# A gated block of two attentions: half of the second head's K moved ahead of a wait, VectorE's sums put behind pairs of GpSimd's, and two constants of the order's planner

## The chip, the cores and the metric

The kernel runs on one core of a Trainium2 chip. The core has five engines that work side by side, each through its own list of instructions in order: TensorE (PE in the profile, with PEld for its weight loads), VectorE (DVE), ScalarE (ACT), GpSimd (POOL), and SyncE (SP), which here only starts transfers. The metric is the time of one execution on the device in microseconds (us), lower is better. The kernel before takes 4916.66 us (median of three runs, 4911.18 to 4921.75).

## The reference

For each of 8 batches, x is 1024 rows of 512 and the context is 1024 rows of 384, all in float32. The block is two attentions one behind the other, each behind a layernorm and each added to x.

```python
x = x + tanh(g_xattn) * xattn(layernorm(x), ctx)   # 8 heads of 64, K and V from the context
x = x + tanh(g_ffn)   * ffn(layernorm(x))          # 16 heads of 32, K and V from x itself

# xattn: softmax(q k^T / 8) v, then @ Wo + bo
# ffn:
q_norm   = q / norm(q, axis=-1)
q_scaled = (q_norm + query_embedding) * softplus(temperature)
h   = softmax(q_scaled k^T / sqrt(32)) v
out = h * gates(h)      # gates: softmaxes of h @ Wr.T, top 3 of 15, and of h @ Ws.T
return out @ Wp.T + bp
```

## The kernel before

**Tiling.** The 512 columns of q and k are cut into 4 chunks of 128, each with 2 heads of 64 (kind 1, the first attention) or 4 heads of 32 (kind 2, the second). In each batch the chunks of kind 1 come first, then `between` finishes the first attention, forms the second's layernorm and its transpose y2T and starts the projections, and then the chunks of kind 2 run. Inside a batch they are called one, two, three and the fourth in the code. The 1024 query columns are handled in two halves of 512, `h` = 0 and 1.

**One chunk.** Four kinds of work belong to it:
- *Projections* (L319 to L395): q and k of each half, four products of four column tiles each (`MM`, one product of the inner loop, is planned at 950 ns). For kind 2 the norm of q follows: ScalarE adds the bias (qq, L355), GpSimd squares it (rn, L356), TensorE sums the squares over a head (pn, L379), ScalarE forms the inverse root (L380, L381), GpSimd multiplies (L382), ScalarE scales (L389).
- *Maxima* (L406 to L472): bfloat16 copies of k and q are made by GpSimd (kb, qb, L398), TensorE forms the scores a first time in bfloat16 (pm, L413), and VectorE takes each row's maximum (mx, L454; L437 in the wide form, which `pace` uses). The maxima then go through a transpose (pr, L465) and a small transfer into the row `sh`, from which the shift of the softmax is added by a product with ones. A chunk of kind 2 has 32 steps of maxima ("pairs") and two closing steps.
- *Scores and values* (L478 to L512, L587 to L626): TensorE forms shift plus scores (sc, L500), ScalarE takes the exponential into a tile e of 128x1024 (L511), TensorE multiplies by v (av, L598). A chunk of kind 2 has 8 steps per half, each with two e tiles, u = 0 and 1.
- *Sums* of the softmax. GpSimd adds two e tiles (`paired`, L516). The result is either added by VectorE to a running sum (L529) or kept as a further term. TensorE then adds up all terms that were kept, with a product by ones (sum, L549). So a result that VectorE does not take costs TensorE time instead. At most 5 e tiles may be held as terms (`room`, L677); when they are too many, the oldest waiting sum is emitted at once (`now`), and if none waits, TensorE sums what there is into a part (L562).

**The order.** The order on TensorE, ScalarE, VectorE and GpSimd is the order in which the program emits instructions. While it emits, it keeps planned clocks: `at["PE"]`, `at["DVE"]` and `at["POOL"]`, in ns, moved on by a planned duration at each instruction (`pe`, `dve`, `pool`). Work that should not be emitted yet waits in two lists, `soon` and `later`, each item with a planned due time; `due` (L666) emits from the head of each list what is due. A sum of VectorE goes into `later` with GpSimd's planned end of that addition (L517, L518).

**The pacing.** During the scores of a chunk, `attend` (L717) mixes in the maxima of the next chunk (and of the one after it, `ahead`) and fillers such as projections. `pair` (L705) emits one step of maxima only where VectorE's planned clock is not too far ahead of TensorE's. `in_time` (L744) compares the planned work of the maxima still to do with the time left in the chunk. Where it says no, VectorE takes no sums in chunks of kind 2 (`ontime`, used in `add` at L523), and TensorE has to sum instead. `pace` (L1049) does the same between the two attentions, where no scores run.

**Around the change.** `between` (L992): the output projection of the first attention for 8 row tiles, each followed by layernorm, a round trip through memory (`put`, `get`) and VectorE's transpose into y2T (`turn`, L1011; L242). The first chunk's projection is begun while the last three tiles are still being turned (L1031 to L1036): q and k of half 0 need tiles 0 to 3 alone, q and k of half 1 need tiles 4 to 7. Then come the first tile of V (L1037, L1038), the rest of the first chunk's projection (L1039), and, in `pace`, the projections of the second and third chunk and the rest of V.

Of the kernel before, what the change touches and what calls it, by code (L numbers as in the profile page):

```python
# [21 lines left out]
def tile_gated_block(  # L22
# [41 lines left out]
    NT = N // P  # L64
    ND = D // P
# [15 lines left out]
    work = ctx.enter_context(tc.tile_pool(name="work", bufs=2))  # L81
# [174 lines left out]
    at = {"PE": 0.0, "DVE": 0.0, "POOL": 0.0}  # L256
    WIDE, MM, PAIR, FOUR, TR, SUM, EXP = 700, 950, 300, 350, 800, 1000, 2100
# [12 lines left out]
    def dve(ns):  # L270
        at["DVE"] = max(at["DVE"], at["PE"]) + ns
# [24 lines left out]
    class Chunk:  # L296
# [19 lines left out]
            if "q" in what:  # L316
                self.wq = load_wc(wq, self.c, f"wq_{self.key}")

        def project(self, st):  # L319

            self.q = qk.tile([P, N], F32, tag="q", name=f"q_{self.key}", bufs=3)
            self.k = qk.tile([P, N], F32, tag="k", name=f"k_{self.key}", bufs=3)
            self.qb = qk.tile([P, N], BF16, tag="qb", name=f"qb_{self.key}")
            self.kb = qk.tile([P, N], BF16, tag="kb", name=f"kb_{self.key}")
            self.waiting = True
            halves = range(NH)
            if self.kind == 1:
                for h in halves:
                    yield from self.project_k(st, h)
                soon.append((at["PE"] + 3000, self.copied, self.kb, self.k))  # L330
                for h in halves:
                    yield from self.project_q(st, h)
            else:
                for h in halves:
                    yield from self.project_q(st, h)
                    yield from self.project_k(st, h)
                    yield from self.norms(h)
                soon.append((at["PE"] + 1000, self.copied, self.kb, self.k))
            soon.append((at["PE"] + 3000, self.begin_maxima))
# [180 lines left out]
        def add(self, h, s, u, a, last):  # L520

            accs = self.acc.setdefault((h, u), [])
            wanted = self.kind == 1 and self.b or ontime[0]  # L523
            free = at["DVE"] <= at["PE"] + 1000
            if accs and not forced[0] and not (wanted if free else wanted and last):
                later.insert(0, (at["PE"] + 300, self.add, h, s, u, a, last))
                return
            elif accs and wanted:
                nc.vector.tensor_tensor(accs[-1], accs[-1], a, ALU.add)  # L529
                dve(1750)  # L530
                live[0] -= 1
                ready = at["DVE"] + 500
            else:
                accs.append(a)
                ready = at["PE"]
            if last and s + 1 == self.ns:
                later.append((ready, self.summed, h, True))
# [49 lines left out]
        def value(self, step):  # L587

            h, s = step
            width, st = self.width, self.st  # L590
            if s == 0:
                self.av = ps_av.tile([P, H], F32, tag="av", name=f"av_{self.key}_{h}")
            e = self.e[step]
            for kk in range(self.nk):
                kc = s * self.nk + kk
                for i in range(self.nh):
                    j = kk * self.nh + i
                    nc.tensor.matmul(  # L598
                        self.av[ts(i, width), :],
                        lhsT=st.v[:, kc, ts(self.c * self.nh + i, width)],  # L600
                        rhs=e[j // 2][:, j % 2, :],
                        start=(kc == 0),
                        stop=(kc == NT - 1),
                    )
                pe(1000)
                if kk == 0 and self.kind == 1:
                    room(1, self, h)
                    self.paired(h, s, 0, e[0], e[1], True)
                if kk + 1 < self.nk:
                    yield  # L610
            if self.kind == 2 and s + 2 == self.ns and self.ends:
                for u in range(2):
                    self.whole[h, u] = [e[u], self.e[h, s + 1][u]]
                live[0] += 4
                later.append((at["PE"] + 3000, self.summed, h, True))
            elif self.kind == 2 and s % 2 == 0:
                room(2, self, h)
                for u in range(2):
                    self.paired(h, s + 1, u, e[u], self.e[h, s + 1][u], u == 1)
            if s == self.ns - 1:  # L620
                nc.scalar.copy(st.hT[h][:, self.c, :], self.av)
                self.divided(h)
            if s % 2 or self.kind == 1:
                self.e.pop(step)
                self.e.pop((h, s - 1), None)
            yield "valued"  # L626
# [27 lines left out]
    later, soon = [], []  # L654
# [34 lines left out]
    def beside(a, b, n=1):  # L689

        while a or b:
            for g in [a] * n + [b]:
                if g and next(g, "end") == "end":
                    a, b = (None if g is a else a), (None if g is b else b)
                elif g:
                    yield

    def run(g, ns):

        end = at["PE"] + ns  # L700
        while g and at["PE"] < end:
            if next(g[0], "end") == "end":
                g.pop(0)
# [13 lines left out]
    def attend(  # L717
        ch, after, first, fillers, cost, maxima=None, ahead=None, since=0.0, rate=1.1, least=300
    ):

        filled, attended = 0.0, 0.0
        columns[0] = ch.width
        total = len(ch.steps) * (ch.SC + 1000 * ch.nk)

        def fill():
            nonlocal filled
            was = at["PE"]  # L730
            while fillers:
                if next(fillers[0], "end") == "end":
                    fillers.pop(0)
                elif ch.kind == 2 or not part[0]:
                    break
            filled += max(at["PE"] - was, least if at["PE"] - was < MM else 0)

        def pairs(slack):
            due(at["PE"])
            if maxima and maxima.mx:  # L740
                return pair(maxima, slack)
            return bool(ahead and ahead.done + 3 < ahead.pairs and pair(ahead, slack))

        def in_time(share):  # L744

            if not maxima or not (maxima.mx or maxima.waiting):
                return True
            pairs = maxima.pairs - maxima.done
            work = pairs * 1450 + 1750 + max(0, at["DVE"] - at["PE"])
            steps = (1 - share) * len(ch.steps) * (2 if ch.kind == 2 else 3)  # L750
            return pairs < 2 or pairs <= steps - 3 and work <= (1 - share) * (1.1 * total + cost) - 7000

        was = at["PE"]
        for got in ch.attention(after, first):
            attended += at["PE"] - was
            share = max(0, attended / total - since) / (1 - since)
            ontime[0] = in_time(attended / total)
            due(at["PE"])
            if got == "begun":
                fill()  # L760
            while got == "valued" and fillers and filled < cost * min(1, rate * share):
                pairs(0)
                fill()
            pairs(1100)
            while got == "ready" and (maxima.mx or maxima.waiting or fillers):
                if not pairs(1100):
                    if fillers:
                        fill()
                    else:
                        at["PE"] += 100  # L770
            was = at["PE"]
        if fillers and since:
            due(1e12)
        run(fillers, 1e9)
        columns[0] = HD2
# [73 lines left out]
    def v2(st):  # L849
        for t in range(NT):  # L850
            ps = gen(f"pv2_{st.b}_{t}")
            yield from product(
                ps, lambda k, t=t: st.yT[:, k, ts(t, P)], lambda k: st.wv[:, k, :], ND
            )
            nc.scalar.copy(st.v2[:, t, :], ps)  # L855
            nc.gpsimd.tensor_tensor(st.v2[:, t, :], st.v2[:, t, :], bv_b, ALU.add)  # L856
            pool(1270)
            yield
# [133 lines left out]
    def between(st, nxt):  # L992
# [25 lines left out]
        one, two, three = st.chunks[2][0:3]  # L1018
# [14 lines left out]
        three.loads()  # L1033
        for t in range(NT - 3, NT):
            turn(t)
            run(fill, 3 * MM)  # L1036
        values = v2(st)  # L1037
        run([values], ND * MM)  # L1038
        run(fill, 1e9)  # L1039
        fill = [two.project(st), beside(values, put1(nxt), ND) if nxt else values]  # L1040
        if nxt:
            fill.append(fetch(nxt, wv1, "wv1"))
        fill.append(three.project(st))
# [135 lines left out]
```

## Time and profile before

| | before |
|---|---|
| time, median of 3 runs | 4916.66 us (4911.18 to 4921.75) |
| time of the profiled execution | 4917.12 us |
| its span, first to last instruction | 4915.3 us |
| TensorE busy | 4754.1 us (97%) |
| VectorE busy | 3112.0 us (63%) |
| GpSimd busy | 2567.6 us (52%) |
| ScalarE busy | 2254.5 us (46%) |
| mean granted TensorE clock | 0.989 |

How to read the lines: a group of instructions is named by its line in the kernel, its engine and its operation, then out<-in with shapes, the count, its busy time and the mean duration of one, and the idle time of the engine just before. A line of the waits gives who waited for whom, then total us, how many times, and the longest. A line of a timeline gives the start in us, the duration in us of a run of like instructions, and in brackets the idle time before it with what ended it. A line of a table by stretches gives the stretch, its length, the busy time and count of instructions, the granted TensorE clock (1.00 is full), the share of transfers and their rate. One product of four column tiles in float32 shows as 8 matmul records.

### The profile page before, as it was taken

How to read it: one execution, taken by the hardware profiler on the slowest of the kernel's cores; microseconds unless marked ns; L12 is line 12 of the kernel's file. 1: busy time of each engine (PE TensorE's matmuls, PEld its weight loads, DVE VectorE, ACT ScalarE, POOL GpSimd, SP SyncE). 2: the span in 40 equal slices, each digit the busy share in tenths (PEclk: the TensorE clock that was granted, in tenths of full speed). 3: DMA queues.
4: the chain of work that ended last, by engine and by line, in shares of the span. 5: the costliest groups of instructions: out<-in, count | busy, mean ns of one | idle time of the engine just before them, and what ended most of it. 6: DMA issues, size and time to landing. Idle time of an engine off the chain costs nothing.

```text
span 4915.3 us, 83941 instructions
## 1 busy us (share of the span) xinstructions
PE 4754.1 (97%) x35196; PEld 1422.8 (29%) x35196; DVE 3112.0 (63%) x4225; ACT 2254.5 (46%) x2916; POOL 2567.6 (52%) x1346
## 2 busy tenths in 40 slices
PE   9999999999999999999999999999999999999998
PEld 2222232222322223222232222322223222232232
DVE  4557665576656865557655576555765567655664
ACT  3435634355343553435534355343552436524364
POOL 1635646366363663636636366363663636636474
PEclk9999999999999999999999999999999999999999
DMA  2020010200103001030010300102002020010100
GB/s 80 27 94 23 26 50 27 95 24 24 50 27 103 16 24 50 29 102 14 24 59 24 99 14 24 65 22 95 14 24 66 26 90 14 17 52 28 34 1 18
DMA packets 212683, 208.12 MB, mean 42 GB/s; under 512 B 24144, under 2 KB 147024, under 8 KB 212304
## 3 DMA queue, kind: packets, MB, share of 16 engines
q1 hardware_dynamic: 212016, 202.76, 13.0%
q8 instruction: 275, 4.51, 0.4%
q14 instruction: 104, 0.85, 0.1%
q10 hardware_dynamic: 288, 0.00, 0.0%
HBM read 153.93 MB, written 48.23 MB: 41 GB/s over the span
## 4 chain that ended last, share of the span: by engine, by line
PE 77%; DVE 12%; issue 3%; POOL 3%; ACT 2%; DMA 2%; SPq 1%; DVEq 0%; ACTq 0%; POOLq 0%
PE sc L500 20%; PE av L598 17%; PE po L282 9%; PE pq L282 8%; PE pm L413 7%; PE pk L282 6%; PE pv L282 5%; DVE mx L454 4%; DVE mx L437 4%; PE sum L549 4%; DVE e L529 3%; POOL e L516 2%; ACT e L511 1%; PE pn L282 1%; SPq L469 1%
## 5 line engine op out<-in xcount | busy, mean ns | idle before, releaser
L516 POOL TENSOR_TENSOR e<-e,e 128x1024 f32<-128x1024 f32 x764 | 1859.3, 2449 | 1122.9 <-PE av L598 660.4
L511 ACT ACTIVATE e<-sc 128x1024 f32<-128x1024 f32 x1536 | 1492.6, 1021 | 1222.7 <-PE sc L500 1186.0
L454 DVE TENSOR_REDUCE mx<-pm 128x1 f32<-128x512 f32 x2332 | 1484.8, 684 | 752.7 <-PE pm L413 709.0
L500 PE MATMUL sc<-q,k 32*128 32x512 f32 (+1 forms) x6144 | 1191.4, 604 | 0.0
L598 PE MATMUL av<-e,v 128*32 128x512 f32 (+1 forms) x6144 | 1086.2, 616 | 0.0
L529 DVE TENSOR_TENSOR e<-e,e 128x1024 f32<-128x1024 f32 x427 | 812.7, 1914 | 347.6 <-POOL e L516 346.7
L413 PE MATMUL pm<-kb,qb 32*128 32x512 bf16 (+1 forms) x3072 | 629.3, 383 | 64.9 <-DVE mx L454 34.4
L437 DVE TENSOR_REDUCE mx<-pm 128x2 f32<-128x1024 f32 x370 | 427.9, 1218 | 280.2 <-PE pm L413 280.2
L500 PEld LDWEIGHTS sc<-q,k 32*128 32x128 f32 (+1 forms) x6144 | 477.2, 189 | 205.5 <-issue 192.4
L500 PE MATMUL sc<-sh,ones_b 1*128 1x512 bf16 x3072 | 411.6, 385 | 32.3 <-ACT e L511 16.5
L413 PEld LDWEIGHTS <-qb 32*128 32x128 bf16 (+1 forms) x3072 | 152.7, 92 | 939.7 <-issue 929.3
L598 PEld LDWEIGHTS av<-e,v 128*32 128x32 f32 (+1 forms) x6144 | 194.0, 117 | 613.7 <-issue 594.5
L282 PE MATMUL pq<-y2T,wq 128*32 128x512 f32 x2048 | 259.5, 625 | 24.6 <-DVE y2T L242 21.8
L282 PE MATMUL pq<-y1T,wq 128*32 128x512 f32 (+1 forms) x1568 | 249.7, 600 | 6.5 <-ACT r L573 2.6
L282 PE MATMUL pv<-wv,y2T 128*32 128x512 f32 x2048 | 243.8, 602 | 2.6 <-DMA wv<-in_L_ffn_Wv 2.6
L282 PE MATMUL pk<-y2T,wk 128*32 128x512 f32 x2048 | 243.2, 595 | 0.0
L282 PE MATMUL po<-wp,h2T 128*64 128x512 f32 (+1 forms) x1152 | 231.1, 595 | 0.0
L282 PE MATMUL po<-wo,h1T 128*32 128x512 f32 x2048 | 223.0, 593 | 0.0
L500 PEld LDWEIGHTS <-ones_b 1*128 1x128 bf16 x3072 | 103.0, 91 | 386.4 <-issue 363.1
L549 PE MATMUL sum<-e,ones 128*32 128x512 f32 (+1 forms) x1380 | 209.7, 595 | 0.2 <-POOL e L516 0.2
L282 PE MATMUL pk<-ctx,wk 128*32 128x512 f32 (+1 forms) x1176 | 189.7, 606 | 19.6 <-DMA ctx<-in_ctx 6.0
L856 POOL TENSOR_TENSOR v<-v,bv_b 128x512 f32<-128x512 f32 x64 | 81.8, 1278 | 239.0 <-ACT v L855 239.0
(110 smaller groups left out, 2784.0 us busy)
## 6 DMA issues: line engine op xcount, KB each, us to landing
y<-xn SPq DMA_DIRECT2D x120, 256.0 KB
xb<-y SPq DMA_DIRECT2D x480, 64.0 KB
x<-in_x SPq DMA_DIRECT2D x64, 256.0 KB
out<-x SPq DMA_DIRECT2D x64, 256.0 KB
xs<-in_x SPq DMA_DIRECT2D x56, 256.0 KB
xn<-in_x SPq DMA_DIRECT2D x56, 256.0 KB
ctx<-in_ctx SPq DMA_DIRECT2D x7, 1536.0 KB
wq<-in_L_xattn_Wq SPq DMA_DIRECT2D x32, 256.0 KB
```

What stands on the lines that cost most here:

```text
L282: nc.tensor.matmul(ps[ts(j, w), :], lhsT=lhsT[:, ts(j, w)], rhs=rhs, start=start, stop=stop)
L413: nc.tensor.matmul(ps, lhsT=self.qb[ts(i, width), ts(c, P)], rhs=self.kb[ts(i, width), ts(kh, H)], start=True, stop=True,)
L437: nc.vector.tensor_reduce(out, tiles[u], AX.X, ALU.max)
L454: nc.vector.tensor_reduce(mx[:, i * NT + c, kh : kh + 1], ps, AX.X, ALU.max)
L469: nc.sync.dma_start(out=self.sh[r : r + 1, :].rearrange("o (c q) -> o c q", c=NT), in_=rows[ts(r // width, NT), :],)
L500: nc.tensor.matmul(pss[u][:, j % 2, :], lhsT=lhsT, rhs=rhs, start=(m == 0), stop=(m == 1))
L511: nc.scalar.activation(e[u], pss[u], AF.Exp)
L516: nc.gpsimd.tensor_tensor(one, one, two, ALU.add)
L529: nc.vector.tensor_tensor(accs[-1], accs[-1], a, ALU.add)
L549: nc.tensor.matmul(ps[ts(2 * u + j, self.width), :], lhsT=ones[:, 0 : self.width], rhs=acc[n][:, j, :], start=(n == 0), stop=(n == len(acc ...
L598: nc.tensor.matmul(self.av[ts(i, width), :], lhsT=st.v[:, kc, ts(self.c * self.nh + i, width)], rhs=e[j // 2][:, j % 2, :], start=(kc == 0 ...
L856: nc.gpsimd.tensor_tensor(st.v2[:, t, :], st.v2[:, t, :], bv_b, ALU.add)
```

## The change

There are four edits.

1. `project` is split: its allocations move into `placed`, and a new `first_k` allocates a chunk's tiles and projects k of half 0 alone. `project`, run later for the same chunk, leaves that half of k out. In `between`, the second chunk's `first_k` (4 products) now stands after the first chunk's norm of half 0, ahead of its q of half 1. The first tile of V, which stood inside q of half 1, is no longer emitted there; it joins the rest of V in `pace`.
2. In `value`, after both of GpSimd's additions of a step of kind 2, the due times of both sums in `later` are set to GpSimd's planned end of the second one.
3. The planned duration of a sum of VectorE falls from 1750 to 1400 ns, in `add` and in `in_time`.
4. The reserve that `in_time` keeps grows from 7000 to 9500 ns.

```diff
-        def project(self, st):
-
+        def first_k(self, st):
+
+            self.placed()
+            yield from self.project_k(st, 0)
+
+        def placed(self):
             self.q = qk.tile([P, N], F32, tag="q", name=f"q_{self.key}", bufs=3)
             self.k = qk.tile([P, N], F32, tag="k", name=f"k_{self.key}", bufs=3)
             self.qb = qk.tile([P, N], BF16, tag="qb", name=f"qb_{self.key}")
             self.kb = qk.tile([P, N], BF16, tag="kb", name=f"kb_{self.key}")
             self.waiting = True
+
+        def project(self, st):
+
+            begun = self.waiting
+            if not begun:
+                self.placed()
             halves = range(NH)
...
                 for h in halves:
                     yield from self.project_q(st, h)
-                    yield from self.project_k(st, h)
+                    if h or not begun:
+                        yield from self.project_k(st, h)
                     yield from self.norms(h)
...
                 nc.vector.tensor_tensor(accs[-1], accs[-1], a, ALU.add)
-                dve(1750)
+                dve(1400)
...
                 for u in range(2):
                     self.paired(h, s + 1, u, e[u], self.e[h, s + 1][u], u == 1)
+
+                later[-2:] = [(at["POOL"], *item[1:]) for item in later[-2:]]
...
-            work = pairs * 1450 + 1750 + max(0, at["DVE"] - at["PE"])
+            work = pairs * 1450 + 1400 + max(0, at["DVE"] - at["PE"])
             steps = (1 - share) * len(ch.steps) * (2 if ch.kind == 2 else 3)
-            return pairs < 2 or pairs <= steps - 3 and work <= (1 - share) * (1.1 * total + cost) - 7000
+            return pairs < 2 or pairs <= steps - 3 and work <= (1 - share) * (1.1 * total + cost) - 9500
...
         for t in range(NT - 3, NT):
             turn(t)
-            run(fill, 3 * MM)
-        values = v2(st)
-        run([values], ND * MM)
+            run(fill, (3 if t + 1 < NT else 1) * MM)
+        run([two.first_k(st)], 1e9)
         run(fill, 1e9)
-        fill = [two.project(st), beside(values, put1(nxt), ND) if nxt else values]
+        fill = [two.project(st), beside(v2(st), put1(nxt), ND) if nxt else v2(st)]
```

## The prediction

> **What bounds the kernel.** The page's first part and its costliest groups come first.
>
> ```profile
> PE 4754.1 (97%) x35196; PEld 1422.8 (29%) x35196; DVE 3112.0 (63%) x4225; ACT 2254.5 (46%) x2916; POOL 2567.6 (52%) x1346
> ...
> L529 DVE TENSOR_TENSOR e<-e,e 128x1024 f32<-128x1024 f32 x427 | 812.7, 1914 | 347.6 <-POOL e L516 346.7
> ```
>
> TensorE sets the time: 4754.1 of 4915.3 us. The change can win only what TensorE waits (161 us), what it does slowly, and the sums it need not do. VectorE's sums take 1914 ns on average and wait 346.7 us for GpSimd, which matters only where TensorE waits in turn. The view of who waited for whom, TensorE's part, says where:
>
> ```profile
> PE pm L413 <- DVE mx L454: 34.4, 76, 2.0
> ...
> PE pq L282 <- DVE y2T L242: 21.8, 8, 4.0
> PE sc L500 <- ACT e L511: 16.5, 17, 2.9
> ...
> PE pk L282 <- DVE mx L454: 4.9, 7, 0.7
> ...
> PE pv L282 <- DMA wv<-in_L_ffn_Wv: 2.6, 3, 1.5
> ```
>
> The second line, once a batch, is edit 1's target; the first, third and fourth hang on VectorE's queue, which edits 2 to 4 reorder. (I leave mx L437, 24.0 us in 88 short waits of the wide form, as it is: no edit touches it.) A wait costs more than its length. The granted clock in stretches after three waits of one batch:
>
> ```profile
> 1508.00:1512.00 4.00, 2.10 (x12) 0.68 (x16) 0.71 (x1) 0.92 (x2) 1.26 (x1) 0.73 0.81 242
> 1512.00:1516.00 4.00, 4.00 (x36) 1.02 (x32) 0.00 (x0) 0.00 (x0) 0.00 (x0) 0.84 0.45 171
> ...
> 1672.00:1676.00 4.00, 3.71 (x20) 0.69 (x19) 1.80 (x4) 0.76 (x1) 1.61 (x1) 0.71 0.00 0
> ```
>
> The third number from the right is the clock. The first two rows lose (1 - 0.73) x 4 + (1 - 0.84) x 4 = 1.7 us. I take 1.7 us for each such spell; tabled in stretches of 4 us, the run has some three a batch, 53 us in all, which the mean clock of 0.989 confirms (0.011 x 4915 = 54).
>
> **Edit 1, half of K ahead of q.** TensorE's timeline between the attentions of one batch, then GpSimd's:
>
> ```profile
> 1506.51 1.07 PE L282 MATMUL pn<-rn,hsum 128*32 128x512 f32 x8
> 1509.90 3.56 PE L282 MATMUL pq<-y2T,wq 128*32 128x512 f32 x16 [2.33 <-DVE y2T L242]
> 1513.28 3.62 PE L282 MATMUL pv<-wv,y2T 128*32 128x512 f32 x32
> ...
> 1522.72 3.62 PE L282 MATMUL pq<-y2T,wq 128*32 128x512 f32 x32
> 1526.16 3.62 PE L282 MATMUL pk<-y2T,wk 128*32 128x512 f32 x32
> ```
>
> ```profile
> 1525.66 1.04 POOL L398 CAST kb<-k 128x1024 bf16<-128x1024 f32 x1
> 1526.64 1.04 POOL L398 CAST qb<-q 128x1024 bf16<-128x1024 f32 x1
> 1527.64 1.04 POOL L356 TENSOR_TENSOR rn<-qq 128x512 f32<-128x512 f32 x1
> ```
>
> *Removed:* the wait of 2.33 us for the last transpose. Four products of k take 3.44 us (1526.16 less 1522.72), and their inputs (y2T's half 0, a weight loaded at the start of `between`) are long there. Of the eight waits six are 2.3 to 2.5 us and vanish; 3.99 and 3.65 leave 0.8 us together. So -21.0 us. The first tile of V, which waited 2.6 us in all for its weight, moves into `pace`, some 12 us later: -2.6. The work itself is only moved: 4 products out of `pace`, 4 in. Its ScalarE copy and GpSimd addition move with it into a stretch where both have room (GpSimd is 52% busy); the transfer of wv keeps its place on SP, and the third chunk's weight loads, queued behind a buffer that frees when the first chunk's q is done, can start some 4 us sooner (1518.4 before, some 1514.4 after).
>
> *Added, though the diff shows it only as a line left out:* in `pace` the second chunk's k of half 0 stood between its q and its pn. It covered the making of rn. With it gone, pn follows q at once, at 1526.2, and needs rn, which GpSimd ends at 1527.64 + 1.04 = 1528.7: behind the first chunk's kb and qb, which the end of q flushes out of `soon` ahead of it. Nothing can slip in: the first chunk's maxima are planned free only 3.6 us (planned) after q, so no pm is emitted before pn. The wait is 2.5 us and some 0.1 for the signal (the old one began 0.14 after its transpose): 8 x 2.6 = +20.8. Queued behind pn are q of half 1 and then the first pm, which come 2.6 us later than they otherwise would; `pace` ends on its 62 products, so the maxima have slack.
>
> *The clock:* seven of the eight old waits are followed by a slow spell (not the seventh batch), the two long ones by two: 9 x 1.7 = -15.3. Does a new wait of 2.6 us slow the clock too? The row says yes: 2.33 us did. The Trainium skill (TensorE: Matmul & The Clock Gate, Part 1) says that the clock falls to half after an idle window of about 3.4 us; by that rule the new waits would cost nothing and edit 1 would bring 18.1 us. I go by the row: +8 x 1.7 = +13.6. **Edit 1 in sum:** -21.0 - 2.6 + 20.8 - 15.3 + 13.6 = **-4.5 us**; bounds -18 (no slow spell) and +11 (no old spell saved).
>
> **Edit 2, sums behind both pairs.** Lines of GpSimd, VectorE and TensorE in the first chunk of the second attention:
>
> ```profile
> 1659.97 5.65 POOL L516 TENSOR_TENSOR e<-e,e 128x1024 f32<-128x1024 f32 x2 [2.00 <-PE av L598]
> ...
> 1660.17 3.22 DVE L529 TENSOR_TENSOR e<-e,e 128x1024 f32<-128x1024 f32 x1
> 1663.32 2.47 DVE L454 TENSOR_REDUCE mx<-pm 128x1 f32<-128x512 f32 x4
> 1665.72 1.21 DVE L529 TENSOR_TENSOR e<-e,e 128x1024 f32<-128x1024 f32 x1
> ...
> 1664.05 0.37 PE L413 MATMUL pm<-kb,qb 32*128 32x512 bf16 x1 [2.00 <-DVE mx L454]
> ```
>
> A sum that runs beside GpSimd's additions takes 3.22 us, one alone 1.21, and pm waits 2.00 us for maxima queued behind it. Over the run such blocking costs 427 x (1.914 - 1.215) = 298 us of VectorE. With both due at the end of the second addition, most run alone. I counted TensorE's waits that begin within 4.5 us of the end of a sum longer than 1.5 us: 24.0 us of pm, 4.9 of pk, 14.1 of sc (through ScalarE, whose e buffer the sum still holds), 43.0 together; 13 slow spells of the clock follow them, 22 us. That is the upper bound of the gain.
>
> What speaks against it: the Trainium skill (SBUF — State Buffer, "Who interferes with whom") says that a VectorE instruction with two inputs in SBUF contends with a GpSimd instruction that reads SBUF, and that the one that starts first blocks the other for its whole length. The row agrees (1.21 against 3.22). By that rule two sums in a row need 2.42 us between GpSimd's pairs. The gaps in this stretch are 2.0 to 4.4 us (2.00 in the row above), so the second sum is met by the next pair in a minority. By the rule alone, with every second sum blocked, nothing of the 43 would be won; with the gaps as measured, three quarters. I take 0.75 of pm and pk, and 0.3 of sc, which sits where no fillers run and GpSimd has no gap: 18 + 3.7 + 4.2 = -25.9; of the spells 60%, -13. The pairs of sums also hold VectorE 2.4 us at a stretch, ahead of maxima, and e buffers longer: lower bound 0, I take +5 for new short waits. **Sum: -33.9 us**, bounds -65 and +41 (second rival).
>
> **Edits 3 and 4, the constants.** TensorE pays for what VectorE does not take. Records of sums in the second attention's four chunks of one batch (PE first):
>
> ```profile
> 1666.10:1734.00 67.90, 3.97 (x32) 0.93 (x32) 0.00 (x0) 1.78 (x3) 0.97 0.03 8
> 1734.00:1801.00 67.00, 7.60 (x64) 2.08 (x64) 1.38 (x2) 1.17 (x2) 1.00 0.14 40
> ```
>
> If all were taken there would be 16 records (two groups of 8, some 0.86 us each by the products' rate). The third chunk keeps nearly all, the second half. The test in `in_time` gets harder by 2500 - 350 = 2150 ns, 1.5 steps of maxima (1450). Against it, each earlier sum is planned 350 ns shorter. The first chunk has 13 sums in its stretch, ten of them of kind 2: 3500 ns, 2.5 steps (1380 each) done ahead. Net one step, so the second chunk should take two sums more, one group a batch: 8 x 0.86 = **-6.9 us**. The third chunk's test fails on its number of steps as well, so it stays. Bounds: two groups gained (-14) and one lost (+7).
>
> **The sum.** 4917.1 (the profiled execution: span 4915.3 and 1.8 around it) - 4.5 - 33.9 - 6.9 = **4871.8**, say 4872. The median of the runs, 4916.7, is 0.4 below that execution, so nothing changes.
>
> **The rivals.**
> - *The waits only move* (0.22). Sums get faster, but pm meets a pair of them instead of one blocked sum, the spells stay and the planner's slack is eaten by edit 4: only edit 1 is left, 4913. For it: two sums in a row take 2.42 us, no less than the 2.2 us of many blocked sums.
> - *Slower: the pairs of sums collide with GpSimd's next pair* (0.16). If both sums come just as it starts, each is blocked for one addition. The place is the first chunk of the second attention, the price that of 1660 to 1673: waits of 2.0 + 1.1 + 0.2 us and a spell of 1.7, so 5 us. One new such place a batch and no gain elsewhere: 4917 - 4.5 + 41 = 4953. There are some 117 pairs of sums (427 less 192 of kind 1, halved); against the forecast's gains it decides from about 12 of them. Against it: the gaps above.
> - *More than forecast* (0.15). All 43 + 22 us go: 4917.1 - 4.5 - 65 - 6.9 = 4841. For it: VectorE is only 63% busy.
>
> **How the numbers follow.** The forecast has 0.47. A measurement of this kernel can tell about 0.2% (10 us) from no change. Faster: 0.47 + 0.15 + 0.06 of the first rival = 0.68; same: 0.14 of that rival; slower: 0.16 + 0.02 = 0.18. The range 4836 to 4925 takes in the third and the first rival with a margin of some 10 us and leaves out the second and a thin lower end. The forecast's own range is 4850 to 4895, from the bounds of edits 2 and 3.
>
> **What would show it.** Edit 1: no wait of pq on y2T over 0.6 us, none of pv on wv, and eight new waits of pn on rn (GpSimd L356) near 2.6 us with a slow clock after. Edit 2: the mean of L529 near 1.4 us, its wait for GpSimd well under 346.7 us, pm on mx L454 near 15. Edits 3 and 4: some 64 fewer of the 1380 sum records. It is wrong if pm's waits stay with fast sums, if the sum records rise, or if pn doesn't wait.

## The result: slower by 2.5%

The changed kernel takes 5036.35 us (median of four runs, 5029.67 to 5048.7) where the kernel before, in the runs beside it, takes 4915.9. The ratio is 1.0251, with a 95% interval from 1.0238 to 1.0264. The forecast was 4872 and its range ended at 4925: wrong in sign and in size. The profiled execution took 5040.7 us, its span is 5038.9, 123.6 more than before.

Lines of the changed kernel stand 11 lower than those of before (L529 is L540, L454 is L465, L500 is L511, L511 is L522). The page's first part and two of its groups:

```profile
PE 4801.6 (95%) x35064; PEld 1438.2 (29%) x35064; DVE 3134.0 (62%) x4250; ACT 2250.2 (45%) x2908; POOL 2560.9 (51%) x1346
...
L540 DVE TENSOR_TENSOR e<-e,e 128x1024 f32<-128x1024 f32 x460 | 835.1, 1839 | 315.6 <-POOL e L527 314.6
...
L560 PE MATMUL sum<-e,ones 128*32 128x512 f32 (+1 forms) x1248 | 205.4, 636 | 2.9 <-DVE e L540 2.7
```

TensorE waits 237 us instead of 161 (span less busy), and is busy for 47 us more. The mean clock fell from 0.989 to 0.979, so 106 us are lost to it instead of 54. So the 124 us are 76 of waiting and 52 of slow clock, less 4 of work. VectorE took 33 sums more and TensorE's sum records fell from 1380 to 1248, as edits 3 and 4 were to bring: the saving came, and something dearer came with it. TensorE's part of the view of who waited for whom:

```profile
PE pm L424 <- DVE mx L465: 62.8, 123, 2.6
PE sc L511 <- ACT e L522: 47.9, 30, 3.9
...
PE pn L282 <- POOL rn L367: 19.1, 8, 2.4
PE sc L511 <- DMA sh<-rows: 18.2, 16, 2.7
```

The first, second and fourth were 34.4, 16.5 and 11.6. The third is the wait forecast for edit 1; the one that edit 1 removes (pq on y2T, 21.8 us) is down to 0.4.

**Where it happens.** I cut each batch where ScalarE copies the last values of a chunk out (h2T, L623 before). One batch's second, third and fourth chunk of the second attention, as a table by stretches, of before and then of after (busy time and count of PE, PEld, DVE, ACT and POOL, then the clock, the transfers' share and rate):

```profile
1666.07:1734.03 67.96, 65.19 (x563) 19.74 (x557) 51.47 (x67) 41.47 (x51) 49.41 (x24) 0.97 0.03 8
1734.03:1800.95 66.92, 65.21 (x553) 20.60 (x549) 42.81 (x67) 38.33 (x45) 41.55 (x20) 1.00 0.14 40
1800.95:1866.29 65.34, 62.00 (x487) 17.14 (x481) 50.25 (x47) 37.52 (x44) 46.54 (x21) 0.97 0.03 8
```

```profile
1699.29:1772.14 72.85, 65.39 (x527) 19.67 (x525) 51.98 (x60) 41.05 (x49) 51.56 (x25) 0.94 0.04 12
1772.14:1847.57 75.43, 69.88 (x567) 22.04 (x567) 44.58 (x72) 38.30 (x45) 41.80 (x20) 0.95 0.11 35
1847.57:1917.38 69.81, 64.02 (x483) 17.25 (x479) 52.71 (x47) 37.30 (x43) 45.83 (x20) 0.94 0.03 8
```

Each chunk is 4.5 to 8.5 us longer, at a lower clock. As a mean of the second to seventh batch the second chunk grew by 4.3 us, the third by 8.5 and the fourth by 4.7; `between` with the first chunk fell by 2.2, and the first attention grew by 0.6: 15.9 us a batch. The third chunk gets the largest part, and no edit acts there: before, it ran almost without VectorE's sums, and it still does. What is new in it are steps of maxima (two pm each). The pm instructions of the same second and third chunk, before and then after (the first time and count are pm's own):

```profile
1666.07:1734.03 67.96, 12.77 (x60) 0.97 0.03 8
1734.03:1800.95 66.92, 13.95 (x54) 1.00 0.14 40
```

```profile
1699.29:1772.14 72.85, 11.24 (x48) 0.94 0.04 12
1772.14:1847.57 75.43, 15.67 (x60) 0.95 0.11 35
```

The third chunk has 6 pm more, the second 12 fewer, and `between` with the first chunk some 6 more (a mean of 150 for 144). Those in the third are the fourth chunk's maxima, which used to be begun in the second. The end of the third chunk shows what they cost. TensorE's timeline of before, from the transpose of the last maxima (pr) to the first scores that need the row sh made from it, with SyncE's line on which the row's four transfers are issued:

```profile
1792.03 0.28 PE L465 MATMUL pr<-ident,nm 128*32 128x128 f32 x1
1792.24 1.06 PE L598 MATMUL av<-e,v 128*32 128x512 f32 x8
1793.26 0.39 PE L500 MATMUL sc<-sh,ones_b 1*128 1x512 bf16 x2
...
1794.28 2.70 SPq L469 DMA_DIRECT2D sh<-rows  x4
...
1795.35 1.06 PE L598 MATMUL av<-e,v 128*32 128x512 f32 x8
1796.35 0.73 PE L500 MATMUL sc<-sh,ones_b 1*128 1x512 bf16 x2
```

And of after, and then two rows of its table by stretches:

```profile
1837.66 0.28 PE L476 MATMUL pr<-ident,nm 128*32 128x128 f32 x1
1837.87 1.06 PE L609 MATMUL av<-e,v 128*32 128x512 f32 x8
...
1838.98 2.70 SPq L480 DMA_DIRECT2D sh<-rows  x4
...
1840.73 0.39 PE L511 MATMUL sc<-sh,ones_b 1*128 1x512 bf16 x1 [1.80 <-DMA sh<-rows]
```

```profile
1840.40:1844.40 4.00, 3.38 (x12) 1.31 (x12) 0.00 (x0) 1.02 (x1) 3.32 (x2) 0.71 0.01 2
1844.40:1848.40 4.00, 4.00 (x22) 0.90 (x20) 0.00 (x0) 1.61 (x2) 0.00 (x0) 0.50 0.00 0
```

The 2.70 us are SyncE's issuing of the four transfers, one after another; when each lands the trace does not tell. Before, a whole step of scores and values (3.1 us, 1792.24 to 1795.35) lies between pr and the scores of the next chunk; these start at 1796.35, 2.07 us after the first transfer was issued, and do not wait. After, the maxima end one step later and that step is no longer between: the scores start at 1840.73, 1.75 us after the first issue, TensorE waits 1.80 and 0.28 us, and the clock then loses 0.29 x 4 + 0.50 x 4 = 3.2 us.

### The profile page after: what moved, and what is told of

Same layout as the page of the kernel before. It is cut to its first block, busy times and chain, and to the rows that moved or that the text cites. A ratio compares the mean times of both kernels' runs of the same rounds, so it can differ in the third digit from the quotient of the medians.

```text
span 5038.9 us, 83805 instructions
## 1 busy us (share of the span) xinstructions
PE 4801.6 (95%) x35064; PEld 1438.2 (29%) x35064; DVE 3134.0 (62%) x4250; ACT 2250.2 (45%) x2908; POOL 2560.9 (51%) x1346
## 4 chain that ended last, share of the span: by engine, by line
PE 77%; DVE 13%; POOL 3%; ACT 3%; issue 2%; DMA 0%; SPq 0%; DVEq 0%; ACTq 0%; POOLq 0%
PE sc L511 19%; PE av L609 17%; PE po L282 9%; PE pm L424 7%; PE pq L282 7%; PE pk L282 7%; PE pv L282 6%; DVE e L540 5%; DVE mx L448 4%; DVE mx L465 4%; PE sum L560 3%; POOL e L527 2%; ACT e L522 1%; PE pn L282 1%; ACT r L584 1%
## 5 line engine op out<-in xcount | busy, mean ns | idle before, releaser
L522 ACT ACTIVATE e<-sc 128x1024 f32<-128x1024 f32 x1536 | 1493.8, 1021 | 1336.0 <-PE sc L511 1232.0
L465 DVE TENSOR_REDUCE mx<-pm 128x1 f32<-128x512 f32 x2332 | 1484.6, 684 | 906.0 <-PE pm L424 849.9
L511 PE MATMUL sc<-q,k 32*128 32x512 f32 (+1 forms) x6144 | 1209.9, 613 | 0.0
L540 DVE TENSOR_TENSOR e<-e,e 128x1024 f32<-128x1024 f32 x460 | 835.1, 1839 | 315.6 <-POOL e L527 314.6
L424 PE MATMUL pm<-kb,qb 32*128 32x512 bf16 (+1 forms) x3072 | 643.8, 386 | 103.6 <-DVE mx L465 62.8
L511 PEld LDWEIGHTS sc<-q,k 32*128 32x128 f32 (+1 forms) x6144 | 485.8, 192 | 203.5 <-issue 188.2
L511 PE MATMUL sc<-sh,ones_b 1*128 1x512 bf16 x3072 | 418.8, 390 | 67.6 <-ACT e L522 47.9
L511 PEld LDWEIGHTS <-ones_b 1*128 1x128 bf16 x3072 | 102.9, 91 | 444.1 <-issue 412.3
L282 PE MATMUL pv<-wv,ctx 128*32 128x512 f32 x1536 | 197.2, 597 | 0.4
```

The costliest lines, as they stand in the source:

```text
L282: nc.tensor.matmul(ps[ts(j, w), :], lhsT=lhsT[:, ts(j, w)], rhs=rhs, start=start, stop=stop)
L424: nc.tensor.matmul(ps, lhsT=self.qb[ts(i, width), ts(c, P)], rhs=self.kb[ts(i, width), ts(kh, H)], start=True, stop=True,)
L465: nc.vector.tensor_reduce(mx[:, i * NT + c, kh : kh + 1], ps, AX.X, ALU.max)
L511: nc.tensor.matmul(pss[u][:, j % 2, :], lhsT=lhsT, rhs=rhs, start=(m == 0), stop=(m == 1))
L522: nc.scalar.activation(e[u], pss[u], AF.Exp)
```

## The experiments

The expectations call a chunk of the second attention a head. Times "a batch" are means of the second to seventh batch against the same stretch of before. Where a run is compared with before, before is the median of the runs beside it.

**Each edit alone.** Edit 1:

```diff
-            run(fill, 3 * MM)
-        values = v2(st)
-        run([values], ND * MM)
+            run(fill, (3 if t + 1 < NT else 1) * MM)
+        run([two.first_k(st)], 1e9)
```

> Edit 1 alone. All theories agree that it is small: the eight waits of q for y2T (21.8 us) and the wait for V's weight (2.6) go, eight waits of pn for rn come (19.1 us in the changed kernel). My forecast says -4.5 us with a slow spell of the clock behind each new wait, -18 without. If edit 1 carried the loss, it would have to be +60 us or more.

Measured: 4904.29 us, ratio 0.9977 (0.9968 to 0.9986), 10.5 us less. The eight new waits of pn are there, 19.1 us. All of it lies in `between` and the first chunk (-1.9 us a batch); the second to fourth chunk are unchanged. Edit 1 is not the cause.

Edit 2 alone:

```diff
+                later[-2:] = [(at["POOL"], *item[1:]) for item in later[-2:]]
```

> Edit 2 alone. Theory P (the planned 1400 ns is the cause: VectorE's queue is promised time that it does not have) expects this one faster than before, by 10 to 40 us, with the mean of a sum near 1.5 us and 434 sums. Theory Q (two sums due together collide with GpSimd's next pair at the seams between heads and hold e tiles; the second rival of the prediction) expects most of the loss here, +60 us or more, with new waits of sc for ScalarE of 20 us or more.

Measured: 4949.51 us, ratio 1.007 (1.0055 to 1.0085), 34.7 us more: neither theory's range. Its waits of TensorE:

```profile
PE sc L500 <- DMA sh<-rows: 37.0, 29, 2.9
...
PE pm L413 <- DVE mx L454: 18.4, 64, 1.5
...
PE sum L549 <- DVE mx L454: 10.7, 7, 1.5
```

Sums that run free do what was forecast for pm: 34.4 us became 18.4. Fewer do than was forecast, though: the mean of a sum fell from 1914 to 1797 ns, not to some 1400; it is 1.28 us (1.83 before) in the stretch of `between` and the first chunk, from which the forecast was read, but still 2.58 (2.53) in the fourth. And the wait for the row sh rose from 11.6 to 37.0 and a new one of 10.7 stands before TensorE's sums, both end on VectorE's maxima: sh is made from them, and TensorE's sums wait for one. The third chunk has 58 pm where before has 53, and is 4.1 us longer.

Edit 3 alone:

```diff
-                dve(1750)
+                dve(1400)
...
-            work = pairs * 1450 + 1750 + max(0, at["DVE"] - at["PE"])
+            work = pairs * 1450 + 1400 + max(0, at["DVE"] - at["PE"])
```

> Edit 3 alone: 1400 ns in the planned duration and in the test of time. The order has 457 sums instead of 427, three more in each second head. Theory P expects most of the loss here, +60 us or more, with the granted clock near 0.98. Theory Q expects within 20 us of before, since no sum's due time is moved.

Measured: 5007.56 us, ratio 1.0187 (1.0172 to 1.0202), 92.8 us more: most of the loss. It runs 457 sums where before runs 427. The third chunk grew by 7.6 us a batch with 60 pm, the fourth by 4.1, the second by 2.4.

Edit 4 alone:

```diff
-... (1.1 * total + cost) - 7000
+... (1.1 * total + cost) - 9500
```

> Edit 4 alone: the reserve of 9500 ns. The order has 423 sums instead of 427. Both theories expect within 10 us of before.

Measured: 4912.91 us, ratio 0.9993 (0.9985 to 1.0002): no difference. The four edits alone add up to -10.5 + 34.7 + 92.8 - 1.9 = +115, against +120 for the whole change, so they can be explained one by one.

**More sums by another road.** Kernel before with a smaller reserve, so that VectorE takes more sums with the old duration and the old due times:

```diff
-... (1.1 * total + cost) - 7000
+... (1.1 * total + cost) - 4000
```

> The kernel before with a reserve of 4000 ns instead of 7000 and nothing else: 462 sums (before 427, edit 3 alone 457), at the old planned duration and the old due times. Theory D (the extra sums in the second head displace maxima of the heads to come into the third, which has no room for them, so its row of maxima ends late, its transfer is waited for and the clock falls) expects the loss of edit 3 here too, +50 us or more, with the third head's stretch near 74 us. Theory P (the planned 1400 ns itself lets TensorE run ahead of VectorE) expects within 25 us of before.

Measured: 5011.9 us, ratio 1.0206 (1.0186 to 1.0225). Without the shorter duration and without the pairs of sums, 462 sums cost as much as edit 3: the second chunk grew by 5.8 us and the third by 6.0, with 62 pm. Only the fourth chunk (+0.4) is spared, where edit 3 has +4.1.

**Fewer sums as a cure.** Edit 3 with a large reserve, and edit 2 with a middling one:

```diff
-                dve(1750)
+                dve(1400)
...
-... (1.1 * total + cost) - 7000
+... (1.1 * total + cost) - 17000
```

> Edit 3 with a reserve of 17000 ns: the planned duration is 1400, but only 416 sums are taken (edit 3 alone 457, before 427). Theory D expects most of the 92 us of edit 3 to go: within 30 us of before, of which 5 us are six more groups of TensorE's sums. Theory P expects +60 us or more, since the planned duration is as wrong as before.

```diff
+                later[-2:] = [(at["POOL"], *item[1:]) for item in later[-2:]]
...
-... (1.1 * total + cost) - 7000
+... (1.1 * total + cost) - 12000
```

> Edit 2 with a reserve of 12000 ns: sums behind both pairs, 423 of them (edit 2 alone 434, before 427). If edit 2 costs its 35 us by the same displacement of maxima (theory D), this is within 15 us of before, 5 us of them for six more groups of sums. If it costs them by collisions with GpSimd's next pair and by held e tiles (theory Q), +25 us or more stay.

Measured: 5053.43 us (1.0275, 1.026 to 1.029) with 416 sums, and 5029.7 us (1.023, 1.0215 to 1.0245) with 423. Both are worse than with the old reserve. So "VectorE takes too many sums" is not the cause as I had put it. Both have 60 pm in the third chunk and lose 8.2 and 8.1 us there, like the changed kernel. That turned the question from the number of sums to where the maxima go.

**The maxima alone.** Kernel before, in which the second chunk may run at most two steps of the fourth chunk's maxima ahead; due times and constants are those of before (the planner then gives VectorE 406 sums for 427):

```diff
+            return bool(ahead and ahead.done < most and ahead.done + 3 < ahead.pairs ...
...
+        attend(two[1], two[2], ..., two[3], rate=1.6 if nxt else 3, most=2)
```

> Kernel before, with one thing changed: during the second head of the second attention at most two of the fourth head's steps of maxima are run ahead. No edit of the change is in it. Displacement theory (what lengthens the third head is how many steps of the fourth head's maxima are left to it, and how near its end they finish; sums only matter by displacing them): the third head gets some 60 records of maxima per batch where before has 53, grows by 5 to 8 us per batch, with a wait for the shifted row at its end and a lower clock behind it, while the second head gets no longer; 4950 to 4980 us. Sum theory (VectorE's sums themselves cost the time, by blocking or by their length): fewer maxima in the second head and no more sums in it leave the time within 10 us of before, 4905 to 4925.

Measured: 4986.55 us, ratio 1.0142 (1.0127 to 1.0158), 72 us more. The second and third chunk of the same batch:

```profile
1689.07:1756.27 67.20, 65.25 (x555) 19.73 (x551) 48.03 (x61) 41.62 (x50) 49.09 (x24) 0.97 0.03 8
1756.27:1827.75 71.48, 67.53 (x561) 21.34 (x557) 44.18 (x71) 38.51 (x45) 42.14 (x21) 0.96 0.13 37
```

The second chunk is as long as before (+0.1 a batch), the third grew by 5.0 with 60 pm, and its end waits 2.4 us for the row sh. The fourth grew by 4.3, which I had not expected, and the first attention of the next batch by 2.4; these are why the time lies above the range given. No edit of the change is in this kernel: moving steps of maxima from the second chunk to the third, and what the planner then orders otherwise, costs 72 us. Of these some 40 (5.0 x 8) lie in the third chunk, where the moved maxima arrive, and at most some 10 are TensorE's own (12 records of sums more a batch, all in the fourth chunk, 1.3 us).

**The maxima brought back.** The changed kernel, with the fourth chunk's projection run earlier in the second, so that its maxima can begin earlier:

```diff
-        attend(two[1], two[2], False, [two[3].project(st)], 18.5 * MM, two[2], two[3], rate=1.6 if nxt else 3)
+        attend(two[1], two[2], False, [two[3].project(st)], 18.5 * MM, two[2], two[3], rate=3)
```

> Kernel after with the fourth head's projection run earlier in the second head (its pace factor 3 for 1.6), so that the maxima that need it can begin earlier there. Displacement theory: fewer records of maxima are left to the third head (some 54 for 60), its wait for the shifted row at the end goes, and it falls back from 75.7 us towards 68 to 70; 4985 to 5005 us, with the number of sums as high as in after. Sum theory: the sums are the same, so the third head stays within 1.5 us of 75.7 and the time within 15 us of 5036.

Measured: 4996.25 us, ratio 1.0165 (1.0148 to 1.0182), 40 us less than the change without it. Its second and third chunk:

```profile
1688.00:1766.45 78.45, 69.56 (x537) 20.51 (x533) 60.83 (x66) 41.44 (x50) 53.69 (x25) 0.96 0.04 12
1766.45:1834.39 67.94, 65.86 (x553) 20.90 (x551) 44.60 (x68) 38.27 (x45) 42.13 (x21) 1.00 0.14 39
```

The third chunk falls from 75.7 to 67.9 us a batch, the fourth from 69.2 to 64.1, both as in before, with 467 sums, more than ever. The second chunk pays: +10.5 us a batch instead of +4.3. The early projection costs some of that in itself, as the run below shows.

**The second chunk.** The changed kernel with at most seven of the second chunk's own sums on VectorE (`n_sums` counts them):

```diff
             wanted = self.kind == 1 and self.b or ontime[0]
+            if self.kind == 2 and self.c == 1 and self.n_sums >= 7:
+                wanted = False
```

> Kernel after, with at most seven of VectorE's sums in the second head of the second attention, as many as before has there (after has 11); the four others go to TensorE. If the number of sums makes the second head's waits (7.4 us idle per batch against 2.5 in before), its idle time falls to about 3 us and the head's length stays near after's 72.5 us or falls by up to 2 us, since TensorE takes 16 records of sums back at some 0.22 us each. If it is where the sums stand (two close behind a pair, held up at the change of heads), the idle time stays at 6 us or more and the head grows to 75 us. The third head, to which one or two steps of maxima fewer are left and whose maxima end some 1 us further from its end, falls from 75.7 us to between 69 and 74 us. In sum 4990 to 5030 us.

Measured: 4962.36 us, ratio 1.0111 (1.0092 to 1.013), 74 us less than the change and below the range given. The limit took less away than I had expected: the stretch has 9 sums instead of 11 (two of each are the first chunk's last ones), and the whole run 445 instead of 460. (A record of a sum takes TensorE about 0.11 us, 3.44 / 32, not the 0.22 written there.) The second and third chunk:

```profile
1675.91:1743.99 68.08, 64.33 (x555) 20.00 (x551) 48.49 (x61) 41.57 (x50) 49.60 (x25) 1.00 0.05 15
1743.99:1813.52 69.53, 66.32 (x549) 20.41 (x545) 43.53 (x70) 38.44 (x45) 41.53 (x20) 1.00 0.14 38
```

The second chunk's idle time falls from 7.4 to 3.7 us a batch, its clock recovers, and pm go back from the third chunk (60 to 56) to the second (46 to 50). The wait for sh at the end of the third is gone (2.2 us to none), and the third chunk is 69.3 us. So at the reserve of the change some sums of this one chunk do displace maxima, and cause its waits too.

**Which sums.** Not their number but their place goes with the displacement. The changed kernel, edit 3 alone and the runs with the reserves 4000, 12000 and 17000 have 8 to 11 sums in the second chunk, three or four of them in its last 21 us, in each of the first seven batches (the eighth is paced otherwise); 60 or 62 pm are then left to the third chunk. Before, edit 1 alone and edit 4 alone have 7 sums there, none of them so late, and leave 52 to 54 pm; the run with seven sums has one so late and leaves 56. By the code, `in_time` says yes as soon as the third chunk's maxima are through, and takes no account of the fourth's. A larger reserve brings that moment forward, since it keeps sums out before it: pr stands 20.2 to 21.8 us before the chunk's end with 17000 and 16.2 to 18.1 with 12000, for 9.7 to 11.6 in before. This fits why larger reserves did not cure it; only the run with seven sums tests it. Two runs show other ways: edit 2 alone has no late sum and leaves 58 pm, and with the earlier projection four late sums go with 54 to 56.

**A better edit 1.** Edit 1 takes the first tile of V out of q of half 1 and thereby uncovers pn. Here the tile goes where the moved half of k stood, so that it covers the making of rn; edits 2 to 4 are left out:

```diff
                 for h in halves:
                     yield from self.project_q(st, h)
-                    yield from self.project_k(st, h)
+                    if h or not begun:
+                        yield from self.project_k(st, h)
+                    else:
+                        for _ in range(ND):
+                            next(st.values)
+                            yield
                     yield from self.norms(h)
```

> Edit 1 alone, and the first tile of V emitted between the second head's q and pn of half 0, where the k that edit 1 moved away stood. It covers the new wait: the eight waits of pn for rn (19.1 us with edit 1 alone) go. If a slow spell of the clock follows each of them, as the prediction had it, 19 + 13 = 32 us less than edit 1 alone (some 4873); if not, 19 us less (some 4886).

Measured: 4881.99 us, ratio 0.9929 (0.9914 to 0.9944), 34 us less than before and the fastest kernel here. Its timeline at the place:

```profile
1508.89 3.64 PE L282 MATMUL pq<-y2T,wq 128*32 128x512 f32 x32
1512.32 3.64 PE L282 MATMUL pv<-wv,y2T 128*32 128x512 f32 x32
1515.90 0.39 PE L428 MATMUL pm<-kb,qb 32*128 32x512 bf16 x4
1516.22 1.06 PE L282 MATMUL pn<-rn,hsum 128*32 128x512 f32 x8
```

The same with the earlier projection of the run above (`rate=3`):

> Kernel before with the K half moved but the first values tile kept between the halves (4882 us alone), and the same earlier projection in the second head as in the run beside it. Displacement theory: two or so records of maxima fewer are left to the third head than in before, which gives back at most 2 us per batch there; 4865 to 4885 us. If the second head has no room for its projection earlier (its own waits for maxima grow), 4890 to 4915.

Measured: 4905.59 us, ratio 0.9982 (0.9974 to 0.9989). The third chunk gains 1.0 us a batch with 50 pm for 53, and the second loses 3.7: in a kernel that displaces nothing there is nothing to bring back.

## Why the prediction was wrong

**Edit 1, "-4.5": right in mechanism, but one term twice too large.** Forecast: eight new waits, 20.8 us; measured 19.1. Forecast: the wait on y2T gone; it is. The whole was -10.5. The difference is in the clock: by the 4 us stretches after the old waits they lost 13.9 us (forecast 15.3), but only four of the eight new waits in the run of edit 1 alone are followed by a slow spell, 6.7 us in all, where I had put 13.6. Which four is a matter of where each wait falls in time (last section), so this term could not have been forecast from the length of a wait. By the rule weighed there (the Trainium skill, TensorE: Matmul & The Clock Gate, Part 1) none would be, and the edit would bring 18.1; the measured 10.5 lies between the rule and the row. So the rule, taken for the length of a wait, does not hold here.

**Edit 2, "-33.9": the term "+5 for new short waits" failed.** The gain counted on pm was 18 us and came to 16. (That is partly luck: the sums did not reach the mean of 1.4 us that was to bring it.) The price of holding VectorE 2.4 us at a stretch, ahead of maxima, was put at 5: it was 25 us of waiting for sh and 11 before TensorE's sums, and slow clock behind them. I had priced a late maximum by pm's wait alone. The maxima also end in a row that a later chunk's first scores need, and that price only shows at the end of the chunk.

**Edits 3 and 4, "-6.9": this step failed.** Forecast: two sums more in the second chunk, one group of 8 records less. Edit 3 alone brought three sums and two groups (16 records a batch there, 1.7 us), so TensorE's saving in that chunk was even larger than forecast; the time rose by 93 us. I had costed what VectorE takes over and left out what it then doesn't do: "the third chunk's test fails on its number of steps as well, so it stays" was right for its sums and overlooked its maxima. Steps no longer run ahead in the second chunk arrive in the third, which has room for them only by ending its maxima one step nearer to the scores that need them.

**The rivals.** The slower one (0.16, 4953 us) had the right sign, and its collision occurs: both sums of a pair blocked by GpSimd. But it stood in the first chunk, where the sums now do run free, and its price was 41 us. In the changed kernel it is found where the second chunk ends and where the fourth begins. Lines of VectorE, GpSimd, ScalarE and TensorE at the end of the second:

```profile
1754.54 5.00 DVE L540 TENSOR_TENSOR e<-e,e 128x1024 f32<-128x1024 f32 x2
...
1756.41 2.05 POOL L409 CAST kb<-k 128x1024 bf16<-128x1024 f32 x1
...
1758.40 2.03 POOL L409 CAST qb<-q 128x1024 bf16<-128x1024 f32 x1
...
1760.40 10.25 POOL L527 TENSOR_TENSOR e<-e,e 128x1024 f32<-128x1024 f32 x4
...
1762.79 3.34 DVE L540 TENSOR_TENSOR e<-e,e 128x1024 f32<-128x1024 f32 x1 [3.26 <-POOL e L527]
1766.23 1.94 ACT L522 ACTIVATE e<-sc 128x1024 f32<-128x1024 f32 x2 [4.50 <-DVE e L540]
1767.30 0.61 PE L511 MATMUL sc<-sh,ones_b 1*128 1x512 bf16 x2 [3.94 <-ACT e L522]
```

The chain reads upwards: TensorE waits 3.94 us for ScalarE, ScalarE 4.50 for the e tile that a sum still reads, the sum takes 3.34 us beside GpSimd's additions, and those are late, in part since kb and qb, copied between the sums, took 2.05 and 2.03 us instead of the 1.04 of before. kb and qb are the fourth chunk's, so its maxima can't start before 1760.4 either, though the third chunk's were done at 1755.4 (pr): from pr to 1767.3 TensorE forms no pm at all. This is a hole in which the maxima that later crowd the third chunk could have run. With the limit of seven sums pr stands 13.5 us before the chunk's end, in the changed kernel 16.7, in before 10.1.

At the start of the fourth chunk two sums in a row are blocked, where before has one of them run ahead of the chunk. VectorE and TensorE, of before and then of after:

```profile
1798.97 3.37 DVE L529 TENSOR_TENSOR e<-e,e 128x1024 f32<-128x1024 f32 x1 [9.16 <-POOL e L516]
...
1806.39 2.24 DVE L529 TENSOR_TENSOR e<-e,e 128x1024 f32<-128x1024 f32 x1
1808.14 0.39 PE L413 MATMUL pm<-kb,qb 64*128 64x512 bf16 x2
```

```profile
1850.67 6.63 DVE L540 TENSOR_TENSOR e<-e,e 128x1024 f32<-128x1024 f32 x2
...
1857.96 0.37 PE L424 MATMUL pm<-kb,qb 64*128 64x512 bf16 x1 [1.53 <-DVE mx L465]
```

The first pm behind the pair wait 1.53 and 0.22 us, and 1.7 us of clock are lost behind them: 3.45 us in each of the second to seventh batch. In the second to seventh batch of all runs this wait and this loss stand exactly where the two sums take 3.3 and 3.4 us, and nowhere where the first of them runs free (1.2 us), as it does in all these batches with the reserve 4000 and in one of them with the capped maxima. So the second rival's mechanism is part of the loss, by this estimate some 28 of the 120 us (8 x 3.45), besides the waits at the second chunk's end.

**What is shown and what isn't.** Shown: displaced maxima lengthen the third chunk in a kernel with none of the edits (5.0 us a batch, within 72 us in all), and undoing the displacement, in two ways, gives back 40 and 74 us of the 120. Shown: limiting the second chunk's sums undoes part of it at the change's own reserve. Argued, with one run for it: that the late sums are what displaces the maxima where the reserve is larger. The fourth chunk's 4.7 us do not follow from the displacement alone: with the reserve 4000 the third chunk has 62 pm and the fourth grows by 0.4. They are for the greater part the pair of blocked sums at its start; why the first of the pair runs free in some runs and batches I have not traced. Nor have I for the 2.4 us of the first attention with the capped maxima.

## What to carry to other kernels

In an order planned ahead, work that one engine takes over pushes other work of that engine along, and the bill comes where the pushed work is needed, here one chunk later and with no edit near it: so follow the displaced steps to the transfer that stands behind the last of them, and count how many steps still cover it. A constant of such a planner should be tried alone, since the order is a fit to it: 350 ns of planned time cost 93 us. And when a wait is filled with work moved from elsewhere, ask what that work was covering there; putting the displaced tile in its place was worth 24 us more than leaving it out.

## What the hardware showed unexpectedly

Waits of the same length do not slow TensorE's clock alike. In the changed kernel the eight waits of pn are 2.38 or 2.39 us each; the 4 us after five of them ran at 0.59 to 0.67, and after the other three at 1.00, and with edit 1 alone it was four and four. The clock's record in the trace shows a pattern: it grants 1.00 or 0.50 and nothing between, and in before, with edit 1 alone and in the changed kernel the slow stretches are 3.41 us long or two or three times that (the last one runs on to the trace's end). The starts of any two of them in one trace lie a whole multiple of 3.413 us apart (in before 42.1, 294.7 and 448.3 us: 74 and 45 times). Cut along this grid, two of the eight waits, the first with a slow clock behind it and the second without:

```profile
1555.38:1558.79 3.41, 1.02 (x12) 0.29 (x12) 0.00 (x0) 1.15 (x2) 2.57 (x3) 1.00 0.00 0
1558.79:1562.20 3.41, 3.41 (x20) 0.87 (x16) 0.00 (x0) 1.38 (x3) 1.27 (x1) 0.50 0.03 5
...
2180.00:2183.41 3.41, 1.57 (x16) 0.32 (x8) 0.00 (x0) 1.50 (x2) 3.41 (x4) 1.00 0.00 0
2183.41:2186.82 3.41, 2.87 (x28) 0.94 (x32) 0.00 (x0) 1.23 (x2) 0.76 (x2) 1.00 0.02 5
```

The first wait lies in one cell of the grid, the second is split, 1.84 us and 0.54. Of the 24 waits at this place (the eight old ones in before, the eight new ones in each of the other two), the 16 that put 2.06 us or more into one cell have half clock in the next, and the 8 that put at most 1.84 us into any do not. It is no general bound: at the start of the fourth chunk 1.75 us in one cell, beside other products, were enough. Where TensorE had waited 1.80 and 0.28 us at the end of the third chunk, the slow stretch is two cells, 6.83 us: 3.4 us lost, double the 1.7 I had taken for a spell. And the blocking of VectorE by GpSimd goes both ways: a copy of 1.04 us took 2.05 beside the sums.
